# Last stage of a fused attention and expert kernel: first tiles' rows in buffers left by earlier stages, first projection inside the last expert block, gathered rows added three pieces later

## The chip, the cores and the metric

The kernel runs on one core of a Trainium2 chip. Five engines take part, each with its own instruction queue, worked off in order: TensorE (PE, matrix products into PSUM), VectorE (DVE), ScalarE (ACT), GpSimd (POOL) and SyncE (SP), which here only issues DMAs. The metric is the device time in microseconds (us), as the median of the runs shown: 1636.28 us over three runs, from 1635.67 to 1639.81.

## The reference

`x` is 4 x 1024 x 512, fp32; attention has 16 heads of 32, the expert layer 8 experts of which each token uses two.

```
xn = layernorm(x)
q, k, v = xn @ Wq.T + bq, xn @ Wk.T + bk, xn @ Wv.T + bv
scores = q @ k.T / sqrt(32), causal, plus the ALiBi bias -slope[h] * |i - j|
attn = softmax(scores) @ v
probs = softmax(xn @ gate_w.T); topw, sel = top_k(probs, 2); topw /= sum(topw)
act = silu(xn @ w1_gate.T) * (xn @ w1_up.T)          per expert
ffn = sum over the two experts of topw * (act @ w2.T)
out = x + (attn @ Wo.T + bo) + ffn
```

## The kernel before

All 4096 tokens lie in 32 tiles of 128 rows. After the layer norm and the routing, two kinds of work are interleaved on PE up to the end.

**Attention** goes through 16 units, one for each of 4 batches and 4 chunks of heads. A unit has twelve groups g0 to g11: g0 to g3 are the four key tiles of the first 512 queries (512, 384, 256 and 128 queries wide), g4 to g11 the eight key tiles of the second 512 (five of width 512, then 384, 256 and 128). A group is a `scores` call (PE products `s`, exponentials `pr` on ACT, on the diagonal groups four masks on POOL), and, in all units but the last, a `largest` call for the next unit (PE products `m`, four or more DVE passes `z`). Before every even group, `values` multiplies the two groups before it with v (PE products `o`) and DVE adds them into `oT`. When a unit's half is complete it is scaled, and for the first three batches stored to `o_d` in DRAM.

**Fills** are the other work, a list of (weight, function) pairs: first 71 expert blocks of 128 token slots each, in pieces `gate`, `up` and `second_layer`, then the final pieces, then `rest`. A planner spreads them: `rate` is the sum of all weights over the number of groups, and `fill` calls, at the end of every group, as many fills as the rate allows. So a weight decides only at which group a piece is issued; the program order that results is kept as it is on every engine (`manual_schedule`). An expert block's `gate(k)` first transposes the previous block's activations (`turn_act`, tile `pact`, copied to `actT` by DVE and ACT), and `second_layer(k)` multiplies the previous block by w2 (`ye`), adds the bias on DVE and stores to `ys_d`. After block 70 there remain a `gate(71)`, which only does `turn_act(70)`, and a `second_layer(71)`, which does `down(70)`.

**Final pieces.** There is one piece for every tile, 32 in all, in the list `order`: the 24 tiles of batches 0 to 2 in turn, with one tile of batch 3 put in at every fourth place (places 3, 7, 11 and so on). I call the latter held places. A piece has these parts:

- `load` issues on SP the DMA of 128 rows of x (`xr`, 256 KB) and, for batches 0 to 2, of the attention's output from `o_d` (`ot`, 256 KB, in runs of 512 bytes). It also issues on POOL two indirect DMAs, `g`, which fetch each token's two expert rows from `ys_d` (256 KB each).
- `piece` runs two DVE `scalar_tensor_tensor` (line 850) that add the gathered rows times `share` to `xr`. For batches 0 to 2 it then calls `project`: eight PE matmuls `y` (line 840), a DVE add (line 843) and the store of `xr` to `out` on SP (line 844). A held place has no projection; its tile waits in one of eight buffers `held` until `rest` projects it straight from `oT`.

The piece at place k first calls `load` for place k + 3 (`ahead = 3`); `prime` loads places 0 to 2. Tiles `xr` and `ot` have four buffers each, `g` has eight. A load into a buffer waits until its former user is done: for `xr` that is the landing of a store. These buffers are in the pool `fin`, opened by `begin_final` in the space of the closed expert pool `ex`, so that the first loads into it also wait for the last expert block's tiles.

Worked out from the weights, the program order of the last two units is as follows. In unit 14, `second_layer(70)` comes in g0; `gate(71)`, `second_layer(71)` and `begin_final` in g1; `prime` in g2; places 0 and 1 in g3, 2 and 3 in g4, 4 and 5 in g5, one place each in g6 to g8, two each in g9 to g11. Unit 15 takes places 15 to 31 and the first four `rest`, and four more `rest` follow at the end.

Of the kernel before, what the change touches and what calls it, by code (L numbers as in the profile page):

```python
# [9 lines left out]
F32 = mybir.dt.float32  # L10
# [6 lines left out]
P = 128  # L17
# [11 lines left out]
def kernel(  # L29
# [18 lines left out]
    T, E = x.shape  # L48
# [4 lines left out]
    NC = E // P  # L53
    NT = T // P
    ST = S // P
    QB = 512
    NQ = S // QB
    QT = QB // P
# [54 lines left out]
    with ExitStack() as actx:  # L113
        wp = actx.enter_context(tc.tile_pool(name="wp", bufs=1))
        qkv = actx.enter_context(tc.tile_pool(name="qkv", bufs=1))
# [8 lines left out]
        def bank(shape, dtype, name):  # L124
            return banks["ring"].tile(shape, dtype, tag="s", name=name)
# [108 lines left out]
        xnT, qs, ks, vs, oTs, mTs = {}, {}, {}, {}, {}, {}  # L234
# [577 lines left out]
        def final_pieces(b):  # L812

            held = {}

            def load(i):
                t = b * ST + i
                xr = phase["fin"].tile([P, E], F32, tag="xr" if b < B - 1 else "held", name=f"xr{t}", bufs=4 if b < B - 1 else ST)
                nc.sync.dma_start(xr, x[t * P : (t + 1) * P, :])
                o = None  # L820
                if b < B - 1:
                    o = phase["fin"].tile([P, NC, P], F32, tag="ot", name=f"ot{t}", bufs=4)
                    cols = slice((i % QT) * P, (i % QT + 1) * P)
                    nc.sync.dma_start(o, o_d[b * NQ + i // QT][:, :, cols])
                gs = []
                for j in range(TOP):
                    g = phase["fin"].tile([P, E], F32, tag="g", name=f"g{t}_{j}", bufs=8)
                    nc.gpsimd.indirect_dma_start(
                        out=g[:, :],
                        out_offset=None,  # L830
                        in_=ys_d[:, :],
                        in_offset=bass.IndirectOffsetOnAxis(ap=slot[:, j, t : t + 1], axis=0),
                    )
                    gs.append(g)
                held[i] = xr, o, gs

            def project(t, xr, lhsTs):
                y = bank([P, E], F32, name=f"y{t}")
                for c in range(NC):
                    nc.tensor.matmul(  # L840
                        y, lhsT=lhsTs[c], rhs=wo_sb[:, c, :], start=(c == 0), stop=(c == NC - 1)
                    )
                nc.vector.tensor_tensor(xr, y, xr, ALU.add)
                nc.sync.dma_start(out[t * P : (t + 1) * P, :], xr)

            def piece(i):
                t = b * ST + i
                xr, o, gs = held[i]
                for j in range(TOP):
                    nc.vector.scalar_tensor_tensor(  # L850
                        xr, gs[j], share[:, t, j : j + 1], xr, ALU.mult, ALU.add
                    )
                if o is not None:
                    project(t, xr, [o[:, c, :] for c in range(NC)])

            def rest(i):
                cols = slice((i % QT) * P, (i % QT + 1) * P)
                project(
                    b * ST + i, held[i][0], [oTs[b, c, i // QT][:, cols] for c in range(NC)]
                )  # L860

            return load, piece, rest

# [251 lines left out]
        def final_all():  # L1117
            ops = [final_pieces(b) for b in range(B)]

            order = [(ops[b], i) for b in range(B - 1) for i in range(ST)]  # L1120
            for i in range(ST):
                order.insert(i * B + B - 1, (ops[B - 1], i))
            ahead = 3

            def prime():
                for ops_, i in order[:ahead]:
                    ops_[0](i)

            res = [prime]
            for k, (ops_, i) in enumerate(order):  # L1130

                def one(k=k, ops_=ops_, i=i):
                    if k + ahead < len(order):
                        nxt, ni = order[k + ahead]
                        nxt[0](ni)
                    ops_[1](i)

                res.append(one)
            return res, ops[B - 1][2]

        phase = {}

# [5 lines left out]
        def begin_final():  # L1148
            phase["ctx"].close()
            phase["fin"] = actx.enter_context(tc.tile_pool(name="fin", bufs=2))  # L1150

        finals, rest = final_all()


        COL = 1.0 / QB
        PROJ, JOIN = 3.6, 1.5
        fills = [(0.0, begin_experts)] + expert_pieces() + [(0.0, begin_final), (3.0, finals[0])]
        fills += [(JOIN if k % B == B - 1 else PROJ, f) for k, f in enumerate(finals[1:])]
        fills += [(PROJ, lambda i=i: rest(i)) for i in range(QT)]

        def unit_todo(n):
# [204 lines left out]
```

## Time and profile before

| what | value |
|---|---|
| median of three runs | 1636.28 us |
| profiled execution, its own time | 1648.37 us |
| profiled execution, span of its instructions | 1646.6 us |
| PE busy over the span | 1612.0 us (98%) |
| DVE / ACT / POOL busy | 939.4 / 890.0 / 332.5 us |

The span runs from the first to the last instruction, and the profiled execution's time is 1.8 us longer than it. That execution is 12.1 us slower than the median of the runs. Times in the views are microseconds from the start of the span. A timeline row has the start, the duration, the engine, the line, the operation, the tiles as out<-in, the shapes and the count; in brackets stands the idle time of the engine before it and what ended that. "SPq" is a DMA issue on SP: its duration is that of the issue and not of the transfer.

From the stage's windows (same execution):

| window, us | PE busy | granted PE clock | DMA share | GB/s |
|---|---|---|---|---|
| 1400 to 1450 | 49.74 of 50 | 1.00 | 0.36 | 118 |
| 1450 to 1500 | 40.77 of 50 | 0.93 | 0.64 | 200 |
| 1500 to 1550 | 48.87 of 50 | 1.00 | 0.76 | 236 |
| 1550 to 1600 | 46.72 of 50 | 0.97 | 0.96 | 314 |
| 1600 to 1647 | 42.62 of 47 | 0.99 | 0.22 | 79 |

### The profile page before, as it was taken

How to read it: one execution, taken by the hardware profiler on the slowest of the kernel's cores; microseconds unless marked ns; L12 is line 12 of the kernel's file. 1: busy time of each engine (PE TensorE's matmuls, PEld its weight loads, DVE VectorE, ACT ScalarE, POOL GpSimd, SP SyncE). 2: the span in 40 equal slices, each digit the busy share in tenths (PEclk: the TensorE clock that was granted, in tenths of full speed). 3: DMA queues.
4: the chain of work that ended last, by engine and by line, in shares of the span. 5: the costliest groups of instructions: out<-in, count | busy, mean ns of one | idle time of the engine just before them, and what ended most of it. 6: DMA issues, size and time to landing. Idle time of an engine off the chain costs nothing.

```text
span 1646.6 us, 29019 instructions
## 1 busy us (share of the span) xinstructions
PE 1612.0 (98%) x9476; PEld 785.9 (48%) x9476; DVE 939.4 (57%) x2886; ACT 890.0 (54%) x2062; POOL 332.5 (20%) x762
## 2 busy tenths in 40 slices
PE   7999999999999999999999999999999999979999
PEld 4545545545454544545544445454444445433333
DVE  6775555655646555555555555555555555547652
ACT  5443455565656465656556474646565565646331
POOL 4610011111020102021111112010211011133660
PEclk9999999999999999999999999999999999999999
DMA  9847854547542434456452335464533424356891
GB/s 312 334 138 255 276 168 155 193 132 237 168 135 89 144 125 146 145 184 209 136 161 88 116 97 174 147 232 153 171 124 105 137 90 156 119 188 200 275 300 64
DMA packets 146486, 278.94 MB, mean 169 GB/s; under 512 B 16448, under 2 KB 45120, under 8 KB 144800
## 3 DMA queue, kind: packets, MB, share of 16 engines
q1 hardware_dynamic: 134384, 234.89, 43.3%
q0 software_dynamic: 10800, 35.40, 7.4%
q10 hardware_dynamic: 1152, 6.82, 1.0%
q8 instruction: 75, 1.23, 0.3%
q14 instruction: 75, 0.61, 0.1%
HBM read 229.07 MB, written 47.97 MB: 168 GB/s over the span
## 4 chain that ended last, share of the span: by engine, by line
PE 88%; DMA 2%; issue 1%; ACT 1%; DVE 1%; SPq 0%; another core or an unknown queue 0%; DVEq 0%; ACTq 0%
PE ye L776 11%; PE pup L728 11%; PE pgate L728 10%; PE s L1007 10%; PE o L1084 8%; PE m L893 8%; PE pk L622 6%; PE pq L622 6%; PE y L840 6%; PE pv L654 5%; PE s L1026 2%; PE pxs L721 2%; PE pact L762 2%; DMA w<-in_w1T 2%; DMA ot<-o_d 1%
## 5 line engine op out<-in xcount | busy, mean ns | idle before, releaser
L1038 ACT ACTIVATE pr<-s,kbias 128x512 f32<-128x512 f32 (+3 forms) x768 | 382.6, 581 | 387.9 <-PE s L1026 345.9
L939 ACT ACTIVATE z<-z,top 128x896 f32<-128x896 f32 (+7 forms) x512 | 391.5, 773 | 84.0 <-DVE top L929 81.0
L1046 POOL TENSOR_SCALAR_AFFINE_SELECT pr<-pr 128x128 f32<-128x128 f32 x512 | 150.4, 302 | 1105.5 <-ACT pr L1038 1099.0
L917 DVE CUSTOM_DVE_ANT_0 z<-m,rel 128x512 f32<-128x512 f32 (+3 forms) x512 | 271.5, 586 | 101.5 <-PE m L893 101.0
L776 PE MATMUL ye<-w,actT 128*128 128x512 f32 (+1 forms) x426 | 197.9, 600 | 2.1 <-DVE actT L765 2.1
L728 PE MATMUL pgate<-w,xsT 128*128 128x352 f32 x568 | 183.9, 464 | 1.8 <-DMA w<-in_w1T 1.4
L728 PE MATMUL pup<-w,xsT 128*128 128x352 f32 x568 | 182.4, 464 | 0.2 <-ACT pr L1038 0.2
L1007 PE MATMUL s<-q,k 32*128 32x512 f32 (+3 forms) x1536 | 179.4, 533 | 0.0
L893 PE MATMUL m<-k,q 32*128 32x512 f32 (+3 forms) x1536 | 172.5, 487 | 4.9 <-DVE oT L1099 4.8
L917 DVE CUSTOM_DVE_ANT_0 z<-m,rel,l 128x128 f32<-128x128 f32 (+3 forms) x256 | 125.8, 547 | 86.6 <-PE m L893 86.1
L1084 PE MATMUL o<-pr,v 128*32 128x512 f32 (+3 forms) x1536 | 144.9, 492 | 0.0
L728 PEld LDWEIGHTS pup<-w,xsT 128*128 128x128 f32 x568 | 105.6, 190 | 68.7 <-ACT pr L1038 9.9
L728 PEld LDWEIGHTS pgate<-w,xsT 128*128 128x128 f32 x568 | 101.5, 190 | 54.3 <-DMA w<-in_w1T 6.2
L622 PE MATMUL pq<-xnT,wq 128*128 128x512 f32 x256 | 119.6, 610 | 1.3 <-ACT pr L1038 0.8
L776 PEld LDWEIGHTS ye<-w,actT 128*128 128x128 f32 (+1 forms) x426 | 76.6, 190 | 90.7 <-issue 72.5
L622 PE MATMUL pk<-xnT,wk 128*128 128x512 f32 x256 | 117.8, 603 | 0.7 <-ACT pr L1038 0.7
L654 PE MATMUL pv<-wv_sb,xnT 128*128 128x512 f32 x256 | 117.0, 600 | 0.2 <-ACT pr L1038 0.2
L1007 PEld LDWEIGHTS s<-q,k 32*128 32x128 f32 x1536 | 61.1, 183 | 108.9 <-issue 82.3
L893 PEld LDWEIGHTS m<-k,q 32*128 32x128 f32 x1536 | 87.2, 185 | 45.5 <-issue 11.7
L745 DVE SCALAR_TENSOR_TENSOR th<-th,pgate 128x352 f32<-128x352 f32 x71 | 37.0, 521 | 121.7 <-ACT th L744 121.7
L939 ACT ACTIVATION_READ_ACCUMULATOR z<-z,top 128x1 f32 x512 | 100.4, 196 | 0.0
L840 PE MATMUL y<-wo_sb,ot 128*128 128x512 f32 x192 | 90.8, 622 | 6.0 <-DMA ot<-o_d 6.0
(165 smaller groups left out, 1564.1 us busy)
## 6 DMA issues: line engine op xcount, KB each, us to landing
w<-in_w1T SPq DMA_DIRECT2D x284, 352.0 KB
w<-in_w2T SPq DMA_DIRECT2D x142, 256.0 KB
ys_d<-yr SPq DMA_DIRECT2D x71, 256.0 KB
w<-in_w2T SPq DMA_DIRECT2D x71, 192.0 KB
xr<-in_x SPq DMA_DIRECT2D x32, 256.0 KB
out<-xr SPq DMA_DIRECT2D x32, 256.0 KB
xn_d<-xT ACTq DMA_DIRECT2D x6, 1024.0 KB
o_d<-oT SPq DMA_DIRECT2D x24, 256.0 KB
```

Of the source, the lines that this page charges most:

```text
L622: nc.tensor.matmul(ps, lhsT=ws[which][:, i, :], rhs=xnT[b, s][:, i, :], start=(i == 0), stop=(i == NC - 1),)
L654: nc.tensor.matmul(ps, lhsT=xnT[b, t // QT][:, i, (t % QT) * P : (t % QT + 1) * P], rhs=wv_sb[:, i, :], start=(i == 0), stop=(i == NC - 1),)
L728: nc.tensor.matmul(ps, lhsT=xsT[k][:, c, :], rhs=w1s[k, c][:, gu, :], start=(c == 0), stop=(c == NC - 1),)
L776: nc.tensor.matmul(y, lhsT=a[:m, f, :], rhs=w2s.pop((k, f))[:m, :], start=(f == 0), stop=(f == NF - 1),)
L840: nc.tensor.matmul(y, lhsT=lhsTs[c], rhs=wo_sb[:, c, :], start=(c == 0), stop=(c == NC - 1))
L893: nc.tensor.matmul(pss[h][:, col : col + n], lhsT=qs[b, c, s][r, (i % QT) * P : (i % QT + 1) * P], rhs=ks[b, c, k0 // QB][r, :n], start=Tr ...
L917: nc.vector.tensor_tensor_reduce(out=zs[h][:, z0 : z0 + n], in0=pss[h][:, col : col + n], in1=rel[:, S - L + k0 : S - L + k0 + n], scale=1 ...
L939: nc.scalar.activation(z[h][:, z0 : z0 + L], z[h][:, z0 : z0 + L], AF.Exp, bias=top[:, h : h + 1], scale=-slopes[c * HC + h], accum_out=to ...
L1007: nc.tensor.matmul(ps[:, :n], lhsT=ks[b, c, j // QT][r, (j % QT) * P : (j % QT + 1) * P], rhs=qs[b, c, s][r, q0:], start=True, stop=False,)
L1038: nc.scalar.activation(pr[:, :n], pss[h][:, :n], AF.Exp, bias=kbias[:, hh, d : d + 1], scale=-slopes[hh],)
L1046: nc.gpsimd.affine_select(out=pr[:, :P], in_=pr[:, :P], compare_op=ALU.is_ge, fill=0.0, base=0, pattern=[[1, P]], channel_multiplier=-1,)
L1084: nc.tensor.matmul(o[h * D : (h + 1) * D, q1:], lhsT=vs[b, j][:, col : col + D], rhs=prs[h][:, : QB - q1], start=(k == 0), stop=(k == len( ...
```

## The change

It touches the final pieces and where they are put, and no arithmetic.

- `load` takes optional buffers. `prime` now loads places 0 to 2 into one `xnT` buffer of attention and into the space of `wv`, both no longer read at that point, and it is put before the last three expert fills, so ahead of `begin_final`.
- The projection of place 0 becomes a fill of its own, put between `gate(71)` and `second_layer(71)`.
- `load` no longer gathers. `gather` is called for places in order, from `begin` (places 0 and 1, after `begin_final`) and from each piece.
- A piece only projects: PE matmuls, then the DVE add of `y` to `xr`. The gathered rows are added by `join`, three places later (fewer at the end, by `late`), and the store follows `join`.
- The piece at place k does, in this order: `join` and the store of place k - 3; `load` of place k + 2; `gather` up to place k + 1 or k + 2; its own projection.
- The weights change: a held place counts 0.6 and not 1.5, `prime` 0 and not 3.0.

```diff
--- before.py
+++ after.py
@@ -813,16 +813,27 @@
 
             held = {}
 
-            def load(i):
+            def load(i, xr=None, o=None):
+
                 t = b * ST + i
-                xr = phase["fin"].tile([P, E], F32, tag="xr" if b < B - 1 else "held", name=f"xr{t}", bufs=4 if b < B - 1 else ST)
+                if xr is None:
...
                 nc.sync.dma_start(xr, x[t * P : (t + 1) * P, :])
-                o = None
                 if b < B - 1:
-                    o = phase["fin"].tile([P, NC, P], F32, tag="ot", name=f"ot{t}", bufs=4)
+                    if o is None:
+                        o = phase["fin"].tile([P, NC, P], F32, tag="ot", name=f"ot{t}", bufs=4)
                     cols = slice((i % QT) * P, (i % QT + 1) * P)
                     nc.sync.dma_start(o, o_d[b * NQ + i // QT][:, :, cols])
-                gs = []
+                held[i] = xr, o
+
+            def gather(i):
+                t = b * ST + i
                 for j in range(TOP):
                     g = phase["fin"].tile([P, E], F32, tag="g", name=f"g{t}_{j}", bufs=8)
                     nc.gpsimd.indirect_dma_start(
@@ -831,8 +842,7 @@
                         in_=ys_d[:, :],
                         in_offset=bass.IndirectOffsetOnAxis(ap=slot[:, j, t : t + 1], axis=0),
                     )
-                    gs.append(g)
-                held[i] = xr, o, gs
+                    held[i] += (g,)
 
             def project(t, xr, lhsTs):
                 y = bank([P, E], F32, name=f"y{t}")
@@ -841,25 +851,32 @@
                         y, lhsT=lhsTs[c], rhs=wo_sb[:, c, :], start=(c == 0), stop=(c == NC - 1)
                     )
                 nc.vector.tensor_tensor(xr, y, xr, ALU.add)
+
+            def store(t, xr):
                 nc.sync.dma_start(out[t * P : (t + 1) * P, :], xr)
 
             def piece(i):
+                xr, o = held[i][:2]
+                if o is not None:
+                    project(b * ST + i, xr, [o[:, c, :] for c in range(NC)])
+
+            def join(i):
                 t = b * ST + i
-                xr, o, gs = held[i]
+                xr, o, *gs = held[i]
                 for j in range(TOP):
                     nc.vector.scalar_tensor_tensor(
                         xr, gs[j], share[:, t, j : j + 1], xr, ALU.mult, ALU.add
                     )
                 if o is not None:
-                    project(t, xr, [o[:, c, :] for c in range(NC)])
+                    store(t, xr)
 
             def rest(i):
+                t = b * ST + i
                 cols = slice((i % QT) * P, (i % QT + 1) * P)
-                project(
-                    b * ST + i, held[i][0], [oTs[b, c, i // QT][:, cols] for c in range(NC)]
-                )
-
-            return load, piece, rest
+                project(t, held[i][0], [oTs[b, c, i // QT][:, cols] for c in range(NC)])
+                store(t, held[i][0])
+
+            return load, gather, piece, join, rest, held
 
 
 
@@ -1123,20 +1140,53 @@
             ahead = 3
 
             def prime():
-                for ops_, i in order[:ahead]:
-                    ops_[0](i)
-
-            res = [prime]
-            for k, (ops_, i) in enumerate(order):
-
-                def one(k=k, ops_=ops_, i=i):
-                    if k + ahead < len(order):
-                        nxt, ni = order[k + ahead]
+
+                o = qkv.tile([P, NC, QB], F32, tag="xnT", name="ot_first", bufs=2)
+                xr = wp.tile([P, NC, E], F32, tag="wv", name="xr_first")
+                for n, (op, i) in enumerate(order[:ahead]):
+                    op[0](i, xr[:, n, :], o[:, :, n * P : (n + 1) * P])
+
+            waiting, unjoined = list(range(len(order))), list(range(len(order)))
+
+            def gathered(upto):
+
+                while waiting and waiting[0] <= upto:
+                    op, i = order[waiting[0]]
+                    if i not in op[5]:
+                        return
+                    waiting.pop(0)
+                    op[1](i)
+
+            def begin():
+                gathered(1)
+
+            def late(k):
+
+                back = (len(order) - 1 - k) // 2
+                return min(back, 3)
+
+            res = [prime, lambda: order[0][0][2](order[0][1]), begin]
+            for k, (op, i) in enumerate(order):
+
+                def join(upto):
+                    while unjoined and unjoined[0] <= upto:
+                        m = unjoined.pop(0)
+                        order[m][0][3](order[m][1])
+
+                def one(k=k, op=op, i=i):
+                    join(k - max(late(k), 1))
+                    if ahead <= k + ahead - 1 < len(order):
+                        nxt, ni = order[k + ahead - 1]
                         nxt[0](ni)
-                    ops_[1](i)
+                    gathered(min(k + 2, unjoined[0] + 3))
+                    if k > 0:
+                        op[2](i)
+                    join(k - late(k))
+                    if k + 1 == len(order):
+                        assert not waiting and not unjoined
 
                 res.append(one)
-            return res, ops[B - 1][2]
+            return res, ops[B - 1][4]
 
         phase = {}
 
@@ -1153,9 +1203,13 @@
 
 
         COL = 1.0 / QB
-        PROJ, JOIN = 3.6, 1.5
-        fills = [(0.0, begin_experts)] + expert_pieces() + [(0.0, begin_final), (3.0, finals[0])]
-        fills += [(JOIN if k % B == B - 1 else PROJ, f) for k, f in enumerate(finals[1:])]
+        PROJ, JOIN = 3.6, 0.6
+        fills = [(0.0, begin_experts)] + expert_pieces()
+
+        fills.insert(len(fills) - 3, (0.0, finals[0]))
+        fills.insert(len(fills) - 1, (PROJ, finals[1]))
+        fills += [(0.0, begin_final), (0.0, finals[2]), (0.0, finals[3])]
+        fills += [(JOIN if k % B == B - 2 else PROJ, f) for k, f in enumerate(finals[4:])]
         fills += [(PROJ, lambda i=i: rest(i)) for i in range(QT)]
 
         def unit_todo(n):
```

More of the change, by code (lines that the diff above doesn't have):

```diff
@@ L814, in final_pieces @@
             held = {}
-            def load(i):
+            def load(i, xr=None, o=None):
                 t = b * ST + i
-                xr = phase["fin"].tile([P, E], F32, tag="xr" if b < B - 1 else "held", name=f"xr{t}", bufs=4 if b < B - 1 else ST)
+                if xr is None:
+                    xr = phase["fin"].tile(
+                        [P, E],
+                        F32,
+                        tag="xr" if b < B - 1 else "held",
+                        name=f"xr{t}",
+                        bufs=4 if b < B - 1 else ST,
+                    )
                 nc.sync.dma_start(xr, x[t * P : (t + 1) * P, :])
-                o = None
                 if b < B - 1:
-                    o = phase["fin"].tile([P, NC, P], F32, tag="ot", name=f"ot{t}", bufs=4)
+                    if o is None:
+                        o = phase["fin"].tile([P, NC, P], F32, tag="ot", name=f"ot{t}", bufs=4)
                     cols = slice((i % QT) * P, (i % QT + 1) * P)
                     nc.sync.dma_start(o, o_d[b * NQ + i // QT][:, :, cols])
-                gs = []
+                held[i] = xr, o
+            def gather(i):
+                t = b * ST + i
                 for j in range(TOP):
```

## The prediction, made before the changed kernel was run

> **What bounds the kernel.** I read the page's busy times first, then its slices.
>
> ```profile
> PE 1612.0 (98%) x9476; PEld 785.9 (48%) x9476; DVE 939.4 (57%) x2886; ACT 890.0 (54%) x2062; POOL 332.5 (20%) x762
> PE   7999999999999999999999999999999999979999
> DMA  9847854547542434456452335464533424356891
> ```
>
> PE is the bound everywhere; the weak slice in the second half (the 36th, 1441 to 1482 us) is the entry into the last stage. So only PE's idle time and its clock can be won or lost. I then listed PE's rows from 1450 us on and looked for bracketed waits:
>
> ```profile
> 1456.19 2.81 PE L776 MATMUL ye<-w,actT 128*128 128x512 f32 x6 [2.06 <-DVE actT L765]
> 1464.40 0.38 PE L1063 MATMUL pi<-mT,pick_inv 128*128 128x512 bf16 x1 [0.64 <-DVE l L917]
> 1466.45 3.67 PE L840 MATMUL y<-wo_sb,ot 128*128 128x512 f32 x8 [1.68 <-DMA ot<-o_d]
> 1470.88 3.67 PE L840 MATMUL y<-wo_sb,ot 128*128 128x512 f32 x8 [0.76 <-DMA ot<-o_d]
> 1482.26 2.07 PE L893 MATMUL m<-k,q 32*128 32x512 f32 x2 [4.01 <-DVE oT L1099]
> 1552.09 5.37 PE L840 MATMUL y<-wo_sb,ot 128*128 128x512 f32 x8 [2.37 <-DMA ot<-o_d]
> 1595.43 3.67 PE L840 MATMUL y<-wo_sb,ot 128*128 128x512 f32 x8 [1.19 <-DMA ot<-o_d]
> ```
>
> Three kinds: the last expert block waits for its own activations; the first projections wait for their loads; two later projections wait for theirs. Two waits also cost clock, read from the windows around them (the busy times of the five engines are followed by the granted clock, the DMA share and GB/s):
>
> ```profile
> 1464.00:1492.00 28.00, 21.15 (x89) 8.37 (x88) 13.04 (x30) 9.70 (x25) 14.82 (x18) 0.88 0.77 254
> 1548.00:1560.00 12.00, 9.63 (x62) 3.83 (x60) 6.26 (x10) 2.96 (x6) 9.51 (x14) 0.86 1.00 325
> ```
>
> 28 x 0.12 = 3.4 us lost after the wait of 4.01, 12 x 0.14 = 1.7 us after that of 2.37 (its eight matmuls take 5.37 instead of 3.67).
>
> **What goes.** (1) The projection of place 0 between `gate(71)` and `second_layer(71)` gives PE 3.6 us of work while `actT` is copied: -2.06. Its inputs are six DMAs of `prime`, issued on SP behind `up(70)` and ahead of the last two blocks' `ys_d` stores and one w2 load. SP issues nothing from about 1445 to 1452 us, so these are not delayed, and the buffers are free (`xnT` of the first half is last read by `pk` at 1387 us, `wv` long before). (2) The waits at 1464.40, 1466.45 and 1470.88 are for loads that had to wait for the pool `fin`; with three tiles loaded early they go: -3.08. (3) The wait of 4.01 with its clock is 7.4 us. Its releaser is a DVE evacuation that itself waited for PE, in a stretch in which POOL issues twelve gathers; no wait that the change removes shows there, and after it eight gathers still come in a row. Bounds 0 and -7.4; nothing in the rows decides, I take half, -3.7. (4) The late loads at 1552 and 1595 belong to an order of loads that is replaced: 2.37 + 1.7 + 1.19 = -5.3. Sum -14.1, at most -17.8.
>
> The DVE passes and stores are as many as before, and adding the gathered rows later costs nothing by itself: gathers are issued three places before their `join`. Dropping held places' weight only shifts work between groups: by the planner's sums the expert blocks now end in g4 of unit 14 instead of g1, and places 13 to 31 stay about where they were. PE's total stays.
>
> **What comes.** The load of place m is moved, and this is where I see the price. Before, SP had for it: store of m-4, then load of m, issued in place m-3. Now it has: store of m-5, load of m, in place m-2. The `xr` buffer that the load takes is, with four buffers and held places skipped, that of place m-5 (m-6 where m-5 is held). Before, another place's store lay between that store and the load. Now, for m = 9, 13, 17, 21, 25 and their successors, the load comes directly behind the store whose landing it needs, that store comes behind `join`, and `ot`, which PE needs, is queued behind `xr` on SP. What such a wait costs is in SP's rows:
>
> ```profile
> 1588.03 0.34 SPq L844 DMA_DIRECT2D out<-xr  x1
> 1588.41 0.43 SPq L819 DMA_DIRECT2D xr<-in_x  x1
> 1588.94 0.52 SPq L824 DMA_DIRECT2D ot<-o_d  x1
> 1590.27 0.34 SPq L844 DMA_DIRECT2D out<-xr  x1
> 1592.33 0.33 SPq L819 DMA_DIRECT2D xr<-in_x  x1
> 1592.75 0.53 SPq L824 DMA_DIRECT2D ot<-o_d  x1
> ```
>
> The first store is place 24's; the load at 1592.33 is place 29's and takes its buffer, 4.3 us after the store's issue. In the same way I find 3.6 (1544.73 to 1548.35) and 3.65 (1498.56 to 1502.21). The nearest quiet row is the last `ys_d` store, 1459.77, whose space is taken at 1462.61: 2.84. I take 3.6, bounds 2.84 and 4.3. From the issue of `ot` to the `y` that waits for it: 3.45 on an empty queue (1463.00 to 1466.45), 6.0 and 6.5 under load (1546.06 to 1552.09, 1588.94 to 1595.43); here SP has just been held, but two gathers run beside it: 4.7, bounds 3.45 and 6.5.
>
> So, from the end of the last projection before the load: DVE add 0.69, `join` 1.53 (two L850 passes), store to load 3.6, `xr` issue 0.43, `ot` 4.7: **10.95 us**. Against it stands what PE has to do until the projection of m. Place m-2 is a held place without a projection, so this is one projection of 3.63 and little else (start-to-start in PE's rows):
>
> - 17: scores of width 384, 1.08, + 3.63 = 4.71; PE waits 6.2
> - 21: width 128, 0.78, + 3.63 = 4.41; 6.5
> - 25: width 512, 1.29, + 3.63 = 4.92; 6.0
> - 13: 1.00 + 3.63 + `o` 0.78 + 1.29 = 6.70; 4.2
> - 9: 1.94 + 3.63 + `o` 1.64 + 0.81 = 8.02. Here DVE must first do the `z` passes of unit 15: as after the `y` at 1521.64, whose L850 starts at 1524.64, `join` begins 1.94 + 3.0 after the last projection, and the chain is 4.94 + 1.53 + 3.6 + 0.43 + 4.7 = 15.2; 7.2
>
> Sum 30.1 us; with both bounds low 20, with both high 43. Place 28, where `late` puts two joins ahead of the load, adds 9.2 - 8.1 = 1.1. Behind the waiting `y` stands all of PE: the next scores, so ACT and the masks too.
>
> Two rules bear on this. The Trainium skill, "DMA: Bandwidth & Descriptors", section Anatomy of one DMA (SWDGE path), has about 2.0 us plus bytes / 436 GB/s for one DMA (fitted on DMAs that GpSimd issues), 2.6 us for 256 KB. With that for both store and `ot` the chain is 7.85, the five waits sum to 14.7, and the kernel ends near 1639. The rows show 3.6 to 6.5 in this stage, where the DMA share is 0.6 to 1.0, so I go by them. Its section Rules for kernel authors says to issue a DMA early and to wait late; the change does that for the gathers and the opposite for `ot`.
>
> "TensorE: Matmul & The Clock Gate", Part 1, halves the clock after an idle window of some 3.4 us, until a busy one has passed. By that a wait of 2.37 is too short; the row shows 1.7 us lost. All five waits are longer: 1.7 each by the row whose wait was for the same load, 8.5; by the row of 4.01 it would be 17.
>
> **Sum.** 30.1 + 1.1 + 8.5 - 14.1 = +25.6 us. On the profiled execution: span 1646.6 to 1672, its time 1648.4 to 1674. The median lies 12.1 us below that execution, and some of its waits may be the profiler's; I carry the same difference over: 1636.3 + 25.6 = **1662 us**. With every bound low (20.1 + 0 + 6.8 of clock for four waits, -17.8): +9, 1645. With every bound high (43 + 2.9 + 17, -10.4): +53, 1689.
>
> **Rivals.**
>
> - **The loads stay hidden; faster.** Gains of 14.1 to 17.8 with no loss: about 1622. For it: before, most loads had 8 to 11 us between issue and use and no wait showed. Against it: it holds only if the chain is under some 4.5 us, and `ot` alone took 3.45 on an empty queue.
> - **Same mechanism at the skill's DMA price**, waits under 4 us, little clock lost: 1639 to 1645. For it: while SP is held, fewer transfers compete. Against it: each store now runs beside two gathers.
> - **The POOL queue.** Gathers now wait for `join` on DVE, and the masks of the next diagonal group are queued behind them: two gathers are 2.5 us, twelve diagonal groups remain, at most 30 us; if half of it reached PE with the loads hidden, 15 - 14 = +1, 1637. Against it: `values` uses a mask one to two groups later, 7 us or more.
> - **The change doesn't do what it says**, if `prime` were held on SP by a buffer: then place 0 stalls the expert end, +3 us more. The free buffers and SP's idle time named above speak against it; I fold it into the first sum.
>
> **Chances.** Late loads at the rows' prices 0.62 (own range 1645 to 1689); at the skill's price 0.18; loads hidden 0.16; POOL queue 0.04. The range 1630 to 1684 leaves out most of the faster case and the top of the first. About 0.3% (5 us) is what a measurement of this kernel can tell from no change: faster 0.16, within 0.07, slower 0.77.
>
> **What will show it.** Right: PE rows of `y` at places 9, 13, 17, 21 and 25 with 4 to 7 us of idle time released by `ot<-o_d`; SP rows where an `xr` load starts 3 us or more after the store just before it; a granted clock under 1.00 in every window of 20 us from 1500 on; no wait before the last `ye`. Wrong: SP's loads directly behind the stores, or `ot` landing before PE comes to it. Then the entry's gain is left and the kernel is faster.

## The result, and the profile after

The changed kernel takes 1675.80 us (median of four runs, 1675.36 to 1680.14) against 1635.97 for the kernel before in the same comparison: ratio 1.0245, 95% interval 1.0221 to 1.0269, some 39.8 us slower. The profiled execution took 1675.52 us, its span is 1673.7.

The page of the changed kernel: PE's busy time, then PE and its granted clock in 40 slices, then the group of the projections (count | busy, mean ns of one | idle before, releaser):

```profile
PE 1618.4 (97%) x9476; PEld 787.1 (47%) x9476; DVE 939.4 (56%) x2886; ACT 890.0 (53%) x2062; POOL 333.1 (20%) x762
PE   7999999999999999999999999999999999996779
PEclk9999999999999999999999999999999999997889
L850 PE MATMUL y<-wo_sb,ot 128*128 128x512 f32 x168 | 90.5, 691 | 34.5 <-DMA ot<-o_d 33.8
```

The weak 36th slice of the kernel before is full now; slices 37 to 39 are weak instead, and there the clock is down too. In the projections' group, 33.8 us of idle time ended with the landing of a projected tile. The windows say the same (PE busy, weight loads, DVE, ACT, POOL, granted clock, DMA share, GB/s):

```profile
1450.00:1500.00 50.00, 49.99 (x306) 21.32 (x308) 32.73 (x103) 31.59 (x74) 17.59 (x27) 1.00 0.61 193
1500.00:1550.00 50.00, 37.17 (x180) 15.86 (x181) 26.02 (x56) 13.84 (x31) 25.09 (x36) 0.83 0.64 196
1550.00:1600.00 50.00, 34.99 (x143) 13.72 (x141) 21.37 (x31) 8.19 (x18) 26.31 (x32) 0.90 0.71 214
1600.00:1650.00 50.00, 43.31 (x198) 17.11 (x199) 20.41 (x29) 11.98 (x24) 16.88 (x28) 0.90 0.56 184
```

The entry of the last stage has next to no idle time (49.99 of 50; it was 40.77), and the 150 us behind it lose more than that: 12.8, 15.0 and 6.7 us. PE's rows of the timeline, those with a wait of over 1 us; the bracket is the wait and what ended it:

```profile
1514.70 9.52 PE L850 MATMUL y<-wo_sb,ot 128*128 128x512 f32 x16 [6.47 <-DMA ot<-o_d]
1537.30 10.18 PE L850 MATMUL y<-wo_sb,ot 128*128 128x512 f32 x16 [6.37 <-DMA ot<-o_d]
1557.30 5.27 PE L850 MATMUL y<-wo_sb,ot 128*128 128x512 f32 x8 [4.93 <-DMA ot<-o_d]
1579.52 6.10 PE L850 MATMUL y<-wo_sb,ot 128*128 128x512 f32 x8 [5.55 <-DMA ot<-o_d]
1602.08 5.07 PE L850 MATMUL y<-wo_sb,ot 128*128 128x512 f32 x8 [5.83 <-DMA ot<-o_d]
1619.82 6.43 PE L850 MATMUL y<-wo_sb,ot 128*128 128x512 f32 x8 [4.62 <-DMA ot<-o_d]
```

The waits stand at places 9, 13, 17, 21, 25 and 28. Eight matmuls without a wait take 3.70 us; behind the waits they take 5.07 to 6.43 (sixteen take 7.13 without a wait, 9.52 and 10.18 here). Before each wait ends a stretch at half clock begins: of 6.83, 10.24, 3.41, 6.83, 3.41 and 6.83 us, in this order. Windows over the first two (the granted clock is the third number from the end):

```profile
1512.73:1519.56 6.83, 4.86 (x6) 2.18 (x7) 0.00 (x0) 0.00 (x0) 1.89 (x2) 0.50 0.90 299
1533.21:1543.45 10.24, 6.16 (x8) 2.54 (x9) 0.00 (x0) 0.22 (x1) 3.83 (x7) 0.50 0.88 295
```

How a wait comes about is in the chain of waits, here from the late sum of one place to the projection of place 9 (start, duration, what):

```profile
1504.77 0.76 DVE xr L867
...
1506.33 2.04 DMA out<-xr
...
1508.38 0.33 SPq L827
...
1508.80 5.76 DMA ot<-o_d
...
1514.70 9.52 PE y L850 x16
```

Sum, store, landing of the store, issue of the input tile, issue and landing of the projected tile: one after the other, with PE idle for the last 6.47 us of it. What SP waits for between 1480 and 1640 us (total, times, longest, us), first in the kernel before, then in the changed kernel:

```profile
SPq L819 <- DMA out<-xr: 2.5, 3, 1.0
```

```profile
SPq L827 <- DMA out<-xr: 52.6, 16, 5.5
SPq L856 <- DVE xr L867: 42.9, 11, 7.8
```

Loads hardly waited for the landing of a store before; now they do so sixteen times.

### The profile page after: what moved, and what is told of

Read it like the earlier page. It is cut to its first block, busy times and chain, and to the rows that moved or that the text cites. A ratio compares the mean times of both kernels' runs of the same rounds, so it can differ in the third digit from the quotient of the medians.

```text
span 1673.7 us, 29017 instructions
## 1 busy us (share of the span) xinstructions
PE 1618.4 (97%) x9476; PEld 787.1 (47%) x9476; DVE 939.4 (56%) x2886; ACT 890.0 (53%) x2062; POOL 333.1 (20%) x762
## 4 chain that ended last, share of the span: by engine, by line
PE 89%; DMA 3%; DVE 1%; ACT 1%; issue 1%; SPq 0%; ACTq 0%
PE ye L776 11%; PE pup L728 10%; PE pgate L728 10%; PE s L1024 10%; PE o L1101 8%; PE m L910 8%; PE y L850 7%; PE pk L622 6%; PE pq L622 6%; PE pv L654 5%; DMA ot<-o_d 2%; PE s L1043 2%; PE pxs L721 2%; PE pact L762 2%; DMA out<-xr 1%; PE pi L1080 1%
## 5 line engine op out<-in xcount | busy, mean ns | idle before, releaser
L850 PE MATMUL y<-wo_sb,ot 128*128 128x512 f32 x168 | 90.5, 691 | 34.5 <-DMA ot<-o_d 33.8
L910 PEld LDWEIGHTS m<-k,q 32*128 32x128 f32 x1536 | 86.7, 185 | 39.8 <-issue 8.2
```

What stands on the lines that cost most here:

```text
L850: nc.tensor.matmul(y, lhsT=lhsTs[c], rhs=wo_sb[:, c, :], start=(c == 0), stop=(c == NC - 1))
L910: nc.tensor.matmul(pss[h][:, col : col + n], lhsT=qs[b, c, s][r, (i % QT) * P : (i % QT + 1) * P], rhs=ks[b, c, k0 // QB][r, :n], start=Tr ...
```

## The experiments

The theories at the start. **Theory 1**: the loads' order costs it all; `ot` comes late because it stands on SP behind an `xr` load that waits for a store just issued. **Theory 2**: adding the rows late costs by itself. **Theory 3**: the entry's parts or the new weights cost.

The runs were made on three chips, in each case with the kernel before on the same chip beside them. The chips differ: the kernel before takes 1635.49, 1649.99 and 1648.39 us on them. So only differences on one chip are compared.

| chip | kernel | median us | against before | ratio (95%) | waits for projected tiles, us |
|---|---|---|---|---|---|
| 1 | before_again (one run) | 1635.53 | 0.0 | | 0 |
| 1 | ot_before_xr | 1649.66 | +14.2 | 1.0079 (1.0060 to 1.0097) | 15.2 |
| 1 | xr_eight | 1664.79 | +29.3 | 1.0180 (1.0163 to 1.0197) | 25.4 |
| 1 | rows_added_at_once | 1639.60 | +4.1 | 1.0028 (1.0017 to 1.0039) | 0 |
| 2 | loads_as_before | 1645.80 | -4.2 | 0.9985 (0.9968 to 1.0002) | 3.7 |
| 2 | late_two | 1671.49 | +21.5 | 1.0143 (1.0109 to 1.0178) | 23.0 |
| 2 | three_then_two | 1671.62 | +21.6 | 1.0139 (1.0106 to 1.0173) | 23.5 |
| 2 | ot_first_xr_eight | 1670.17 | +20.2 | 1.0133 (1.0099 to 1.0166) | 22.6 |
| 3 | after_again | 1685.42 | +37.0 | 1.0229 (1.0206 to 1.0251) | 34.5 |
| 3 | both_earlier | 1663.28 | +14.9 | 1.0098 (1.0075 to 1.0121) | 16.2 |
| 3 | load_before_sum | 1646.57 | -1.8 | 0.9993 (0.9978 to 1.0008) | 3.1 |
| 3 | three_ahead_first | 1641.48 | -6.9 | 0.9956 (0.9940 to 0.9971) | 0.8 |

### The kernel before, once more

No edit. 

> The kernel before once more, for a second profile. The first profiled execution took 1648.4 us, 12 us over the median of its runs, and with it the entry of the last stage showed a PE wait of 4.01 us and half clock behind it. If that wait belongs to the kernel, the second profile has it again near 1480 us and a span of about 1646. If it belongs to that one execution, the span is about 1634 and the wait is missing, and then the change had 7.4 us less to win than the sum counted (3.7 of it taken).

Its span is 1633.7 us, 12.9 below the profile that the prediction was made from. PE's rows from 1450 us on, all that have a wait:

```profile
1456.06 2.82 PE L776 MATMUL ye<-w,actT 128*128 128x512 f32 x6 [2.06 <-DVE actT L765]
1464.27 0.38 PE L1063 MATMUL pi<-mT,pick_inv 128*128 128x512 bf16 x1 [0.64 <-DVE l L917]
1466.52 9.77 PE L840 MATMUL y<-wo_sb,ot 128*128 128x512 f32 x16 [1.87 <-DVE inv L1065]
1507.77 1.12 PE L893 MATMUL m<-k,q 32*128 32x512 f32 x2 [0.76 <-DVE oT L1099]
```

The wait of 4.01 us at 1482 and the late loads at 1552 and 1595 are not there. So the kernel does not have them in every execution. What the change could win here is the first three waits, 4.57 us, and the clock behind them: sixteen matmuls take 9.77 us at 1466.52, where sixteen take 7.13 us elsewhere in the stage.

### The projected tile ahead of the input tile

```diff
-                nc.sync.dma_start(xr, x[t * P : (t + 1) * P, :])
...
                     nc.sync.dma_start(o, o_d[b * NQ + i // QT][:, :, cols])
+                nc.sync.dma_start(xr, x[t * P : (t + 1) * P, :])
```

> The changed kernel with the two DMAs of a load in the other order: ot first, then xr. Theory 1 (the late loads: ot queued behind an xr load that waits for the landing of the store just before it): ot no longer waits for that landing, 2.0 to 2.6 us in the rows of the changed kernel, so each of the six waits before y (sum 33.8) falls to 2.5 to 4.5 us, with less half clock behind it; 1655 to 1664 us. Theory 2 (adding the gathered rows three places later costs by itself, through DVE, the stores and the gathers): no change, about 1676. Theory 3 (the entry and the weights, which press the final pieces into fewer groups): no change, about 1676.

On this chip the kernel before takes as long as in the result (1635.5 and 1636.0 us). Of the +39.8 us, 14.2 stay; the six waits are 1.32 to 3.26 us, 15.2 in all. SP's rows around place 9 show the cure and what it leaves:

```profile
1504.84 0.34 SPq L856 DMA_DIRECT2D out<-xr  x1
1505.28 0.52 SPq L831 DMA_DIRECT2D ot<-o_d  x1
1506.93 0.33 SPq L832 DMA_DIRECT2D xr<-in_x  x1
```

The input tile still waits for the store (issued at 1504.84, taken up at 1506.93), but the projected tile of the same place no longer stands behind it.

### Eight buffers for the input tiles

The space of `xr_first`, unused after place 2, is taken as four more `xr` buffers in turn with the pool's four. The edit, with its helper cut to the core and simplified:

```diff
+            def ahead_load(m):
+                op, i = order[m]
+                n = m - m // B
+                if m % B == B - 1 or n % 8 > 3:
+                    op[0](i)
+                else:
+                    op[0](i, room["xr"][:, n % 4, :], None)
...
-                        nxt, ni = order[k + ahead - 1]
-                        nxt[0](ni)
+                        ahead_load(k + ahead - 1)
```

> The changed kernel with eight xr buffers instead of four (the four rows of the freed wv space are used in turn with the four of the pool), all else as it is. Theory 1: the load's wait for the store just before it goes, 2.0 to 2.6 us of each of six waits, but the load still stands behind that store and so behind join: 1655 to 1664 us, like the run with ot first. Theories 2 and 3: about 1676.

Between 1480 and 1640 us SP's list of waits has no load that waits for a store's landing (16 times in the changed kernel), and yet 29.3 us stay. SP's rows around place 9:

```profile
1507.05 0.34 SPq L856 DMA_DIRECT2D out<-xr_first  x1
1507.44 0.43 SPq L827 DMA_DIRECT2D xr<-in_x  x1
1507.97 0.52 SPq L832 DMA_DIRECT2D ot<-o_d  x1
```

The load follows its store within 0.05 us, and the store itself came only when DVE had done the late sum. Stores wait 94.8 us for late sums in that stretch (60.4 for `xr`, 34.4 for `xr_first`). So the store's landing is not all of it: a first mark against theory 1 as I had put it. Nor are buffers short: loads of projected tiles wait 0.7 us for theirs. The transfers themselves are slower here: the median from the issue of a projected tile to its landing is 7.2 us, against 5.1 in the changed kernel and 5.5 with the projected tile first; why was not tested.

### Rows added in the piece itself

The third part of the change undone, with the loads and gathers three places ahead that go with it; entry and weights stay as changed.

```diff
                 def one(k=k, op=op, i=i):
-                    join(k - max(late(k), 1))
-                    if ahead <= k + ahead - 1 < len(order):
-                        nxt, ni = order[k + ahead - 1]
+                    if k + ahead < len(order):
+                        nxt, ni = order[k + ahead]
                         nxt[0](ni)
-                    gathered(min(k + 2, unjoined[0] + 3))
+                    gathered(k + ahead)
+                    op[3](i)
...
-                    join(k - late(k))
...
+                    if op[5][i][1] is not None:
+                        op[6](i)
```

Here `op[3]` adds the rows, ahead of the projection, and `op[6]` stores behind it.

> The changed kernel with its third part undone: the gathered rows are added in the piece itself, ahead of the projection, and loads and gathers are issued three places ahead, as before the change. The early first rows, the projection inside the last expert block and the new weights stay. Theories 1 and 2: the six waits go and the gain of the entry is left, about 5 us of waits at the entry: 1628 to 1633 us. Theory 3: still slow, above 1655.

The six waits go, and still it is 4.1 us slower than the kernel before. The loss is at the entry, where DVE stands before the gathered rows:

```profile
1476.42 0.75 DVE L867 SCALAR_TENSOR_TENSOR xr_first<-g,share,xr_first 128x512 f32<-128x512 f32 x1 [6.67 <-DMA g<-ys_d,slot]
```

Behind it PE has three waits of 0.86 to 1.03 us, each put down to DVE, and the window from 1450 to 1500 us has a clock of 0.86, where the changed kernel has 1.00. So the first places do need the late sum, and theory 3 is not the loss of 39.8 us.

### Late sums kept, loads three places ahead

Eight buffers for `xr` and, in the same way, for `ot`; place k issues the load of place k + 3, behind the late sum as before:

```diff
-                    if ahead <= k + ahead - 1 < len(order):
-                        nxt, ni = order[k + ahead - 1]
-                        nxt[0](ni)
+                    if k + ahead < len(order):
+                        ahead_load(k + ahead)
```

> The changed kernel with the order of its loads put back: the late adding of gathered rows, the early first projection and the weights stay, but place k issues the loads of place k+3 (as before the change) and the projected tiles and input tiles have eight places each, so that a load never needs a store of the last ten places. Theory 1 (the loads that stand behind a just issued store cost the time, and nothing else of the change does): all six waits for ot in the last block go, the entry stays clean (no half clock between 1450 and 1500), 1624 to 1631 us, faster than the kernel before by 5 to 11. Theory 2 (adding the rows late costs by itself, since each late sum puts two more DVE operations and a store in front of a projection): 1640 or more, although no wait for ot is left. Theory 3 (the entry's parts and the weights cost by themselves): 1640 or more, with the waits between 1460 and 1500.

0.9985, interval 0.9968 to 1.0002: not told from no change, 4.2 us faster where theory 1 expected 5 to 11 (its absolute times were meant for the first chip). Theory 2 falls: all rows are added as late as in the changed kernel, and 3.7 us of waits are left of some 34. The expectation of a clean entry missed: on this chip PE runs 10.24 us at half clock from 1484.6 on, and every kernel profiled on chips 2 and 3 has such a stretch; more on that at the end.

### Two places later in place of three

```diff
-                return min(back, 3)
+                return min(back, 2)
```

> The changed kernel with one number changed: the gathered rows are added two places later in place of three. The sum and store of place m-5 then go out one place before the load that needs its buffer. Theory 1 (a load directly behind the store that frees its buffer): the store has a whole place, some 5 us, to land, so the six waits for ot mostly go (under 6 us left of 33.8), 1628 to 1640 us. Theory 2 (adding late costs by itself, in proportion to how late): about two thirds of the loss stays, 1660 to 1665. Theory 3 (entry and weights): 1670 or more.

And the same from place 6 on only:

```diff
-                return min(back, 3)
+                return min(back, 3 if k < 6 else 2)
```

> The changed kernel with the rows added three places later for places 0 to 5 and two places later from place 6 on. Theory 1: the entry is as in the changed kernel (no half clock between 1450 and 1500) and the stores have a place to land, so 1626 to 1636 us, and not slower than the version with two places throughout. Theory 2 (adding late costs by itself): 1660 or more. Theory 3 (entry and weights): 1670 or more.

Both miss what theory 1 expected: +21.5 and +21.6. The waits move one place, to 8, 12, 16, 20, 21, 24 and 28. In the version with two places throughout, SP's rows and PE's row at place 8 say why:

```profile
1496.05 0.62 SPq L827 DMA_DIRECT2D xr<-in_x  x1
1511.79 0.34 SPq L856 DMA_DIRECT2D out<-xr  x1
1512.17 0.43 SPq L827 DMA_DIRECT2D xr<-in_x  x1
1512.65 0.53 SPq L832 DMA_DIRECT2D ot<-o_d  x1
```

```profile
1518.03 6.25 PE L850 MATMUL y<-wo_sb,ot 128*128 128x512 f32 x8 [4.49 <-DMA ot<-o_d]
```

No landing is waited for between 1511.79 and 1512.65, and in the whole stretch from 1480 to 1640 us only 4.8 us (52.6 in the changed kernel). But SP issued nothing for 15.1 us before (1496.67 to 1511.79), with the load ready behind a store that waited for a sum on DVE; the tile was then 5.4 us under way. Here the order of the queue alone keeps the load late.

### Both cures at once

The projected tile first, and eight buffers for input tiles; the diffs are those above. 

> The changed kernel with both partial cures at once: a place's projected tile is loaded ahead of its input tile, and input tiles have eight places, so that neither the sum of a wait for a store nor the input tile's transfer stands ahead of the projected tile. What is left is that the load is issued two places ahead behind the late sum's store, and that the ot buffer itself has four places. Theory 1, if the two cures add up (26.1 and 11.0 us of the loss each alone): 1638 to 1642 us, waits for ot of 5 to 9 us in all. If the tile's own transfer, issued too late, is what remains (about 5.8 us from issue to landing): no better than with the projected tile first alone, 1645 to 1651.

+20.2 us, 22.6 us of waits: the cures don't add up, since both take away the same thing, the landing in front of `ot`. That it is slower against its kernel before than the projected tile first alone was on another chip I can't explain: at place 9 the waits are alike (3.29 and 3.08), and they part later, most of all at place 21 (5.59; 1.70 at places 20 and 21 together there). With chips changed between the two, it stays open.

Theory 1 is split then. **1a**: two places of lead are too few for the chain. **1b**: standing behind the late sum and its store costs at any lead. (The version with loads three places ahead and eight buffers already speaks against "at any lead": it stands behind the sum and has 3.7 us of waits.)

### One place more of lead

```diff
-                return min(back, 3)
+                return min(back, 2)
...
-                    if ahead <= k + ahead - 1 < len(order):
-                        nxt, ni = order[k + ahead - 1]
+                    if k + ahead < len(order):
+                        nxt, ni = order[k + ahead]
```

> The changed kernel with the late sums and the loads each one place earlier: rows are added two places later, and place k issues the loads of place k+3. Buffers, the store that frees them and the order of the queue are those of the changed kernel (the load still stands behind the store of the place five earlier, which it needs), only the load has one place more before its use. Theory 1a (what costs is the lead: a chain of some 11 us from late sum to landed tile has two places to run in where the kernel before had three): a further place is worth some 5 us, about what each of the six waits lasts, so they shrink to under 6 us in all, and the ratio to the kernel before is 0.998 to 1.006. Theory 1b (what costs is standing behind the late sum and its store, whatever the lead): most of the waits stay, ratio 1.013 or more.

Between the two: of 37.0 us (the changed kernel on this chip) 14.9 stay. The chain is the same as in the changed kernel, landing included, one place earlier; that is worth 22.1 us. Ten waits for projected tiles are left, of 0.36 to 3.39 us, in place of seven of up to 6.79.

### The load ahead of the late sum, two places of lead

Eight buffers for both tiles, and:

```diff
-                    join(k - max(late(k), 1))
                     if ahead <= k + ahead - 1 < len(order):
-                        nxt, ni = order[k + ahead - 1]
-                        nxt[0](ni)
+                        ahead_load(k + ahead - 1)
+                    join(k - max(late(k), 1))
```

> The changed kernel with the load issued two places ahead, as there, but ahead of the late sum of the same place, and with eight places for input tiles and projected tiles, so that it needs no recent store. Theory 1a (lead): the load is held only by the store of the place before, so it leaves the queue one place earlier, most of the time; waits of 0 to 10 us in all, ratio 0.998 to 1.008. Theory 1b (standing behind the late sum and its store): the same or better, 0.996 to 1.002. If waits of more than 15 us stay, neither the store's landing nor the place in the queue was it, and two places are too few for the transfer alone.

-1.8 us, 0.9993 (0.9978 to 1.0008): the whole loss is gone at the changed kernel's own lead of two places. So a lead of two places is enough for the transfer itself; what makes it too few is what stands ahead of the load in SP's queue. Stores still wait 79.5 us for late sums between 1480 and 1640 us, but now behind the load of their place, and no load waits for a landing. Two of the waits that are left, for the price of clock:

```profile
1522.06 3.67 PE L850 MATMUL y<-wo_sb,ot_first 128*128 128x512 f32 x8 [0.38 <-DMA ot_first<-o_d]
1528.92 5.37 PE L850 MATMUL y<-wo_sb,ot_first 128*128 128x512 f32 x8 [2.10 <-DMA ot_first<-o_d]
```

### Late sums, with all that was late put ahead

Loads three places ahead, ahead of the late sum, the projected tile first, eight buffers of both:

```diff
-                    join(k - max(late(k), 1))
-                    if ahead <= k + ahead - 1 < len(order):
-                        nxt, ni = order[k + ahead - 1]
-                        nxt[0](ni)
+                    if k + ahead < len(order):
+                        ahead_load(k + ahead)
+                    join(k - max(late(k), 1))
```

> All that was late put ahead: late sums as in the changed kernel, loads three places ahead, issued before the late sum of their place, the projected tile ahead of the input tile, eight places for both. Theory 1 in both forms: no wait for a projected tile is left (the version with loads three places ahead behind the sum had 3.7 us), 2 to 10 us faster than the kernel before, ratio 0.994 to 0.999. If adding rows late cost by itself, it would be slower than the kernel before, 1.003 or more.

0.9956 (0.9940 to 0.9971), 6.9 us faster than the kernel before and 43.9 faster than the changed one on the same chip. Its page, PE and the clock:

```profile
PE   7999999999999999999999999999999999999999
PEclk9999999999999999999999999999999999998999
```

No weak slice is left between the first and the last; one slice of clock shows the entry's loss on this chip.

### The changed kernel, once more

No edit. 

> The changed kernel once more, on the same chip as the three others, so that what they win of the loss can be read on one chip. All theories: six waits for projected tiles of 30 to 36 us in all, ratio 1.020 to 1.028.

The ratio is as at first (1.0229), and so are the six waits, 6.79 to 4.42 us, of 34.2 together, with 0.2 for a seventh. But the entry, clean in the first profile, is not so here:

```profile
1450.00:1500.00 50.00, 47.44 (x250) 19.79 (x248) 25.96 (x86) 24.91 (x58) 14.36 (x20) 0.90 0.50 156
```

## Why the prediction was right, and where its terms were off

The sign was right and so, in the main, was the mechanism, and 1675.80 lies in the range; the forecast of 1662 is 13.8 us low. By its own steps:

- **What bounds the kernel**: PE, rightly; the loss is PE's idle time and clock and nothing else. From the second profile of the kernel before to that of the changed one, PE's busy time grows by 1618.4 - 1606.3 = 12.1 us for the same matmuls, and its idle time by (1673.7 - 1618.4) - (1633.7 - 1606.3) = 27.9; together the 40.0 us by which the spans differ. All but about one of the 12.1 us is clock: PE is busy for 27.5 us of the six stretches at half clock and for 5.4 us of the one that the second profile of the kernel before has; half of each, 13.7 and 2.7, is what they cost.
- **The wait before the last `ye`, -2.06**: right, gone.
- **The entry's waits, -3.08**: right; the second profile has 0.64 + 1.87 there, with some clock, and the changed kernel none.
- **The wait of 4.01 with its clock, -3.7, and the late loads, -5.3**: wrong for the runs that were timed. The kernel's second profile, which lies at their median, has none of the three waits, so these 9.0 us of the 14.1 were not there to be won. What the entry and the late sums are worth without the loss is the 6.9 us (4.8 to 9.9 by the ratio's interval) of the last version, on another chip, whose kernel before takes 12 us longer.
- **The waits at places 9, 13, 17, 21, 25, 30.1 us**: 6.47, 6.37, 4.93, 5.55 and 5.83, together 29.2, against 7.2, 4.2, 6.2, 6.5 and 6.0. At place 9 the chain's terms were off in opposite ways: 2.04 us and not 3.6 from the store to the load, 5.76 and not 4.7 for the projected tile. (The sign "3 us or more after the store" so failed at these five places, with 2.04 to 2.62.) The largest miss, at place 13, is a term left out: there the late sum stood behind 2.4 us of other DVE passes (1525.12 to 1527.49). That the sum came so near, 29.2 for 30.1, is in part luck.
- **The sixth wait, 1.1**: 4.62, at place 28 as forecast. The term was mis-sized: its tile alone was 6.01 us under way (1613.67 to 1619.69), where the chain had 4.7.
- **The clock, 8.5**: 13.7; mis-sized. The six rows show 2.39, 3.05, 1.57, 2.40, 1.37 and 2.73 above 7.13 or 3.70, 13.5 in all. The 1.7 for each wait was the price of one stretch of 3.41 us; three of the waits had 6.83 us at half clock and one 10.24. In these rows a wait cost about half of what was left of its stretch when it ended: at place 13 half clock begins at 1533.21 and the wait ends at 1537.30, and (10.24 - 4.09) / 2 = 3.08. The Trainium skill, "TensorE: Matmul & The Clock Gate", Part 1, names an idle window of some 3.4 us as what halves the clock. In the version with the load ahead of the sum, a wait of 2.10 us cost 1.70 (5.37 against 3.67), while with the projected tile first one of 2.94 cost none (3.67), and neither did the kernel before's 2.06 ahead of `ye` (2.82 for six matmuls, 2.84 without a wait in the changed kernel). The length of the wait alone decides neither way here.
- **The step that put the forecast 13.8 us low is the carry-over to the median.** Profile against profile, 1646.6 to 1673.7 is +27.1, and the sum had +25.6. But the first number held waits that the kernel's second profile, at the median of the runs, does not have. I took the 12.1 us between that execution and the median over to the changed kernel, and at the same time counted 9.0 us of its waits as a gain; that can't both be. With 4.57 us of waits and the 2.6 us of clock at 1466 as the gain, the sum is 30.1 + 1.1 + 8.5 - 7.2 = +32.5; the sixth wait (3.5 more), the clock (5.2 more) and the five waits (0.9 less) bring it to 40.3, against 40.0 between the spans. That +25.6 lies so near +27.1 is luck in part: the costs were 7.8 us too low, so the gains against that profile must have been some 6 us too low as well.
- **The mechanism as I put it**, the load directly behind the store whose landing it needs, was half of it. Without a landing between a place's store and its `ot`, 14.2 and 29.3 us stay on the first chip and 20.2 on the second. The other half is the place in the queue: the store of the late sum waits on DVE, and the next load waits behind the store. Both halves go with the load ahead of the sum, and with the loads three places ahead, as long as buffers are there. Those two runs change buffers and order together; eight buffers of both with the changed kernel's own order was not tried. But with eight for input tiles alone 29.3 us stay, although loads wait 0.7 us for a projected tile's buffer there and for no store, so buffers by themselves are not the cure.
- **The rivals**: loads hidden (1622) and the low DMA price (1639 to 1645) fall by the six waits; the estimate of 2.6 us for 256 KB from the formula of the Trainium skill, "DMA: Bandwidth & Descriptors", Anatomy of one DMA, is less than half of the 5.76 that `ot` took, and above the 2.04 from the store to the load. The POOL queue showed in no wait of PE.

## What to carry to other kernels

When the consumer of a buffer is moved later, every store behind it moves too, and with it every load that is issued behind that store on the same queue: follow the queue in order, and put the loads ahead of the work that may wait, with enough buffers that a load needs no recent store. Lead counted in places is not lead in time; it begins when the queue comes to the load. Before gains are read off a profile, have a second profile of the same kernel: waits that only one of them shows are not to be counted on.

## What the runs showed that I had not expected

The kernel before takes 1635.5 us on one chip and 1648.4 and 1650.0 on two others, and the changed kernel 1675.8 and 1685.4. All eight kernels profiled on chips 2 and 3 have 6.83 or 10.24 us at half clock that begin between 1483 and 1487 us, with PE's short waits there mostly put down to no other engine ("issue", 1.00 and 1.04 us in the changed kernel). The stretch in the changed kernel, and the second of these waits:

```profile
1483.33:1493.57 10.24, 10.08 (x15) 3.55 (x15) 6.63 (x14) 5.22 (x12) 4.57 (x4) 0.50 0.60 174
1482.44 0.37 PE L1043 MATMUL s<-mT,ones_b 3*128 3x512 bf16 x1 [1.04 <-issue]
```

The profiles of the changed kernel and of the kernel before with a time near 1636 or 1676 have none at that place. What holds PE there was not found. That the first profile of the kernel before, with its 4.01 us at 1482, came from such a chip fits, but its chip is not on record.
